# Turning the norm's deviations by TensorE, and comparing through a second tensor, in the patch-sorting stage of a four-layer network

## The chip, the cores and the metric

The kernel runs on one core of a Trainium2 chip. The metric is device time in microseconds of one execution, as the median of several runs. A profiled execution gives the trace from which all durations below are read. The engines are named as in the profile: PE is TensorE (matmul; PEld its weight loads), DVE is VectorE, ACT is ScalarE, POOL is GpSimd, SP is the queue that issues DMAs.

## What is computed

The input is four images of 128 channels by 64 x 64 pixels. Four layers follow one another. The change lies in the first, cut here to what matters:

```python
sm = final_scores.reshape(B, Hp, PS, Wp, PS).mean((2, 4)).reshape(B, Hp * Wp)
idx = jnp.argsort(-sm, axis=1)                 # 256 patches of 4 x 4 pixels, best first
...
x1 = x_re.transpose(0, 2, 1) + pe_re           # pixels in the order of their patches, plus a position
mu = x1.mean(-1, keepdims=True)
var = ((x1 - mu) ** 2).mean(-1, keepdims=True)
x1n = (x1 - mu) * jax.lax.rsqrt(var + 1e-05) * norm_g + norm_b
xz = x1n @ in_proj_w.T
...
_, ys = jax.lax.scan(step, h0, ...)            # a state-space scan along the 4096 pixels
...
inv = jnp.argsort(order, axis=1)               # the pixels go back to their places
```

The scores come from two depthwise convolutions with a channel attention. The norm is over the 128 channels of a pixel. The layers after it (a convolution, an attention, two expert feed-forwards and a linear attention) are not touched.

## The kernel before, in words

All tensors have the 128 channels on the partitions; a chunk is 512 pixels, eight to an image. For each image `in_order` prepares the sequence: a group norm, two depthwise convolutions on TensorE from patches that went through DRAM, the score of each patch, the sort, the norm, and the permutation of the patches by matmul. `scan` then runs the state-space scan over the image, in eight pieces of 512 columns. A piece has 8 groups (`g`) of two slots (`i`), so 16 slots, and an image 128.

The first image is prepared alone, with every engine free, and there the framework's scheduler places the instructions. From then on the order is written by hand: the scan of image b runs, and beside it `others(b)` prepares image b + 1 as a Python generator that is advanced by one turn in each slot (line 919, pace 1). During the scan of the last image the finished sequences of the first three are put back into place instead (`end`, `put_back`).

In each slot the order of issue is:

- if `i` is 0, VectorE's product `hs` of 128 x 2048 (L886), whose second input `b_ps` comes from PE through one PSUM buffer;
- ScalarE's two `decay` exponentials (L893), through two PSUM buffers;
- `K.flush()` (L895), which issues all that was put off with `later` in the slot before;
- VectorE's two scans (L897), then on GpSimd a small copy of the carry (L900) and the product `hs` by `c_sb`, 128 x 1024 (L901), then on PE the sums `y_ps` of an earlier group;
- one turn of the preparation, and last, if `i` is 0, the next `b_ps` on PE.

Around this, once in each piece, lie the steps of `enter` for the next piece: `xc_ps`, `dbc_ps`, `dt_ps` on PE, activations on ScalarE, `dt` and `sp_u` on VectorE (L799, L800; the profile puts them to L126, the line that calls what was put off), and three products of 128 x 1024 on GpSimd. `leave` closes a piece: `yt` on VectorE (L825) and GpSimd (L821), `out_ps` on PE. `K.bank` gives out PSUM banks in turn (three during the scan) and flushes early when none is free.

The part that changes, for chunk c of the norm:

- `ask` loads the position; `placed` adds it to the image on GpSimd (L612); `centred` subtracts the mean by a matmul (`pos_xc`), and ScalarE squares it (L628) and copies it into `xn`, sorted by place in the patch (L630);
- `varied` takes the mean of the squares by a matmul with the 128 x 128 matrix `K.mean`. Every partition of `pos_var` then holds the same variances, 512 columns. VectorE turns them in blocks of 32 x 32 (L642) and copies one column of each block into `spreads` (L643): 16 numbers per partition and chunk;
- after every fourth chunk ScalarE takes the root (L649) and VectorE the reciprocal (L654); then, chunk by chunk, VectorE turns the 16 numbers, each repeated over 32 columns, back into `ln_rs` of 128 x 512 (L659), and GpSimd multiplies `xn` by it in two halves (L669). `ln_rs` has one buffer for the first four chunks, and alternates with that of `ln_vt` for the last four;
- `turn` and `sorted_` then transpose and permute on PE, with VectorE's copy L691 between, which needs all of `xn`.

`sort` compares each score with all others. `before` (L581) and `perm` (L603) compare the constant row `K.col` of 256 numbers with one number per partition; `eq` and `beats` (L583, L585) have two inputs besides. `put_back` compares in the same form at L947. In each slot's turn the sort's VectorE instructions are issued directly, so they stand behind the slot's scans.

Of the kernel before, what the change touches and what calls it, by code (L numbers as in the profile page):

```python
# [9 lines left out]
F32 = mybir.dt.float32  # L10
F32R = mybir.dt.float32r
I32 = mybir.dt.int32
AF = mybir.ActivationFunctionType
ALU = mybir.AluOpType
# [3 lines left out]
P = 128  # L18
# [3 lines left out]
CH = 512  # L22
NCH = L // CH
# [6 lines left out]
class Common:  # L30
# [59 lines left out]
    def mm(self, out, lhsT, rhs, start=True, stop=True):  # L90
        self.nc.tensor.matmul(out, lhsT, rhs, start=start, stop=stop)  # L91
# [32 lines left out]
    def later(self, f, *args, **kw):  # L124

        self.late.append(lambda: f(*args, **kw))  # L126
# [144 lines left out]
def layers01(K, xd, dpool, w, w1):  # L271
# [3 lines left out]
    nc, tc, mm = K.nc, K.tc, K.mm  # L275
# [5 lines left out]
    with ExitStack() as ctx:  # L281
# [94 lines left out]
        deep1 = depthwise(w["conv1_w"], "deep1")  # L376
        deep2 = depthwise(w["conv2_w"], "deep2")
        rect = lambda t: t.rearrange("p (y x) -> p y x", x=HW)

        def image(b):  # L380
            t = big.tile([P, L], F32, name="xb", tag="mid")
# [6 lines left out]
        def staged(n, period, *stages):  # L388


            active, begun, turn = [], 0, 0
            while begun < n or active:
                if begun < n and turn >= begun * period:
                    active.append([begun, 0])
                    begun += 1
                for a in list(active):
                    if stages[a[1]] is not None:
                        stages[a[1]](a[0])
                    a[1] += 1
                    if a[1] == len(stages):  # L400
                        active.remove(a)
                turn += 1
                yield

        def together(*parts):

            parts = list(parts)
            while parts:
                for p in list(parts):
                    if next(p, True):  # L410
                        parts.remove(p)
                if parts:
                    yield

        def wait(n):
            for _ in range(n):
                yield
# [5 lines left out]
        def in_order(b, made, work, psum):  # L423
# [143 lines left out]
            def sort():  # L567
                yield from wait(6)
                sp = K.bank(psum, [P, 256], "sm_ps")
                mm(sp, share.to_broadcast([P, P]), sm)  # L570
                later(nc.vector.tensor_copy, sm, sp)
                yield from wait(2)
                beats = []
                for h in range(2):
                    dg = small.tile([P, P], F32, name="dg")
                    nc.vector.tensor_tensor(dg, sm[:, h * P : (h + 1) * P], K.ident, ALU.mult)
                    cl = small.tile([P, 1], F32, name="cl")
                    nc.vector.tensor_reduce(cl, dg, AX.X, ALU.add)

                    before = small.tile([P, 256], F32, name="before")  # L580
                    nc.vector.tensor_scalar(before, K.col, K.row[:, h : h + 1], None, ALU.is_gt)  # L581
                    eq = small.tile([P, 256], F32, name="eq", tag="rank_eq")
                    nc.vector.scalar_tensor_tensor(eq, sm, cl, before, ALU.is_equal, ALU.mult)  # L583
                    bt = small.tile([P, 256], F32, name=f"beats{h}")
                    nc.vector.scalar_tensor_tensor(bt, sm, cl, eq, ALU.is_lt, ALU.add)  # L585
                    beats.append(bt)
                    yield
                yield
                rp = K.bank(psum, [P, 256], "rank_ps")
                for h in range(2):  # L590
                    mm(rp, K.ones, beats[h], start=h == 0, stop=h == 1)
                rank = small.tile([P, 256], F32, name="rank", bufs=NB)
                kept["rank"] = rank
                later(nc.vector.tensor_copy, rank, rp)
                yield
                yield
                for h in range(2):
                    dg = small.tile([P, P], F32, name="dg")
                    nc.vector.tensor_tensor(dg, rank[:, h * P : (h + 1) * P], K.ident, ALU.mult)
                    cl = small.tile([P, 1], F32, name="cl")  # L600
                    nc.vector.tensor_reduce(cl, dg, AX.X, ALU.add)
                    pm = small.tile([P, 256], F32, name=f"perm{h}", tag=f"beats{h}")
                    nc.vector.tensor_scalar(pm, K.col, cl, None, ALU.is_equal)  # L603
                    perm.append(pm)
                    yield

# [24 lines left out]

                later(taken)

            spreads = small.tile([P, NCH, CH // 32], F32, name="spreads")

            def varied(c):
                vp = K.bank(psum, [P, CH], "pos_var")
                mm(vp, K.mean, squares.pop(c))

                def turned():  # L640
                    vt = work.tile([P, CH // 32, 32], F32, name="ln_vt", tag="vt", bufs=1)
                    nc.vector.transpose(vt.rearrange("p a b -> p (a b)"), vp)  # L642
                    nc.vector.tensor_copy(spreads[:, c].unsqueeze(2), vt[:, :, 0:1])  # L643
                    if c % 4 == 3:
                        later(root)

                def root():
                    at = spreads[:, c - 3 : c + 1]
                    nc.scalar.activation(at, at, AF.Sqrt, bias=K.eps5)  # L649
                    later(inverted)  # L650

                def inverted():
                    at = spreads[:, c - 3 : c + 1]
                    nc.vector.reciprocal(at, at)  # L654
                    turned_back(c - 3)

                def turned_back(n):
                    rs = work.tile([P, CH // 32, 32], F32, name="ln_rs", tag="vt" if n > 3 and n % 2 else "rs", bufs=1)
                    nc.vector.transpose(rs, spreads[:, n].unsqueeze(2).to_broadcast([P, CH // 32, 32]))  # L659
                    later(scaled, n, rs.rearrange("p a b -> p (a b)"))  # L660
                    if n < c:
                        if n > 3:
                            later(turned_back, n + 1)
                        else:
                            later(later, turned_back, n + 1)

                def scaled(n, rs):
                    for a in range(2):
                        nc.gpsimd.tensor_tensor(inner(n, a), inner(n, a), outer(rs, a), ALU.mult)  # L669

                later(turned)

            yield from together(tail, sort(), staged(NCH, 2, ask, None, placed, centred, None, varied))
            yield from wait(7)


            xq = big.tile([P, L + 3], F32, name="xq", tag=f"seq{b % 2}")
# [262 lines left out]
        def put_back(xb, om, rank, prep, psum):  # L940
# [3 lines left out]
            perm_inv, turned = [], {}  # L944
            for h in range(2):
                pi = small.tile([P, 256], F32, name=f"perm_inv{h}")
                nc.vector.tensor_scalar(pi, rank, K.row[:, h : h + 1], None, ALU.is_equal)  # L947
                perm_inv.append(pi)
            yield

# [1123 lines left out]
```

## Time and profile before

| what | us |
|---|---|
| median of 3 runs | 10186.19 |
| lowest and highest run | 10174.80 and 10188.59 |
| the profiled execution | 10174.38 |
| its span, first to last instruction | 10172.6 |
| preparation of the first image, up to the scan's first L886 | 281.6 |
| scan of images 1, 2, 3 and 4, from first L886 to the next one's | 612.8, 612.1, 614.7 and 650.9 |
| pieces 0 to 7 of the third image's scan | 65.9, 69.3, 74.2, 106.3, 100.6, 73.1, 62.7, 62.6 |

The last two rows were read off the starts of L886 in the trace. In pieces 1 to 3 the convolutions of the next image run beside the scan, in pieces 4 and 5 its sort, norm and permutation, in 6 and 7 nothing. Both other scans that have a preparation beside them show the same lengths within 4 us a piece.

How to read the lines that follow: a group line gives line, engine, operation, output and inputs, shapes and count, then total busy us, mean ns of one, and the idle time just before, with what ended it. A line of the order in time begins with start and duration in us. A line of windows gives the stretch, its length, the busy us and number of instructions of PE, PEld, DVE, ACT and POOL, the granted clock of TensorE, and the DMA share and rate.

### The profile page before, as it was taken

To read this page: it belongs to the slowest core of one execution; us is meant where nothing else is said; L and a number is where in the kernel's file an instruction comes from. 1 tells how busy PE (TensorE), PEld (TensorE's weight loads), DVE (VectorE), ACT (ScalarE), POOL (GpSimd) and SP (SyncE) were. 2 spreads that over 40 slices of the span, in tenths; PEclk is the share of its full clock that TensorE was granted. 3 is DMA by queue.
4 is the path that set the end of the run, shared out by engine and by line. 5 is a ranking of instruction groups with operands and counts; after the bars stand their busy time and mean duration, and the time that the engine had idled before them with its cause. 6 is when DMAs were issued, how large, how long until landed. Compare 5 with 4: busy or idle time off the path is not lost. (4 is left out here: it accounts for less than half of the span.)

```text
span 10172.6 us, 185611 instructions
## 1 busy us (share of the span) xinstructions
PE 8764.2 (86%) x72472; PEld 3315.3 (33%) x72472; DVE 7559.9 (74%) x8255; ACT 7361.3 (72%) x10542; POOL 4791.7 (47%) x3135
## 2 busy tenths in 40 slices
PE   5687887889859999969999969999979999967766
PEld 1122222235433333323333323333333333323433
DVE  1789797997748888868888768888778888753563
ACT  2666656654439999959999959999869999831531
POOL 0667576675515555545555545555445555420000
PEclk8787878889979999989999979999989999988987
DMA  5634536222222222142222142222132222123004
GB/s 125 154 77 104 130 77 149 65 75 76 77 64 36 41 42 38 29 110 35 42 40 39 29 111 35 42 38 39 28 112 38 39 39 40 36 94 118 0 18 149
DMA packets 629614, 669.26 MB, mean 66 GB/s; under 512 B 185400, under 2 KB 416896, under 8 KB 621568
## 3 DMA queue, kind: packets, MB, share of 16 engines
q1 hardware_dynamic: 628736, 657.39, 28.3%
q8 instruction: 571, 9.36, 0.4%
q14 instruction: 307, 2.51, 0.1%
HBM read 446.84 MB, written 143.13 MB: 58 GB/s over the span
## 5 line engine op out<-in xcount | busy, mean ns | idle before, releaser
L1491 ACT ACTIVATE ex<-score 128x1024 f32<-128x1024 f32 x5120 | 4928.0, 1037 | 176.2 <-PE score L91 89.1
L91 PE MATMUL ctx_ps<-ex,qt 128*32 128x512 f32 x20480 | 2735.6, 606 | 19.8 <-DVE ctx L1425 19.8
L1440 POOL TENSOR_TENSOR folded<-ex 128x1024 f32<-128x1024 f32 x512 | 1224.9, 2392 | 2124.8 <-ACT ex L1491 1857.4
L1497 DVE STREAM_TRANSPOSE turned<-ex 128x1024 f32<-128x1024 f32 x1536 | 1886.6, 1228 | 375.6 <-ACT ex L1491 278.6
L1473 DVE STREAM_TRANSPOSE turned<-ex 128x1024 f32<-128x1024 f32 x1532 | 1843.3, 1203 | 0.0
L91 PE MATMUL acc_ps<-turned,turned_v 128*32 128x256 f32 x24576 | 1769.5, 379 | 3.0 <-DVE turned L1503 3.0
L897 DVE TENSOR_TENSOR_SCAN hs<-decay,carry,hs 128x512 f32<-128x512 f32 x1024 | 1245.9, 1266 | 230.3 <-ACT decay L893 217.6
L91 PE MATMUL score<-queries,keys 32*128 32x512 f32 x10240 | 1334.9, 497 | 95.0 <-ACT ex L1491 44.4
L91 PEld LDWEIGHTS acc_ps<-turned,turned_v 128*32 128x32 f32 x24576 | 801.0, 110 | 1476.4 <-issue 1327.1
L901 POOL TENSOR_TENSOR hs<-hs,c_sb 128x1024 f32<-128x1024 f32 x512 | 1207.8, 2359 | 109.0 <-DMA c_sb<-c_d 69.0
L893 ACT ACTIVATE decay<-dt,a_neg 128x512 f32<-128x512 f32 x1024 | 694.3, 689 | 748.0 <-DVE hs L897 737.9
L91 PEld LDWEIGHTS score<-queries,keys 32*128 32x128 f32 x10240 | 512.9, 182 | 1191.8 <-ACT ex L1491 823.1
L1297 POOL TENSOR_TENSOR turned_v<-v,quarter 128x1024 f32<-128x1024 f32 x256 | 612.5, 2393 | 265.1 <-PE acc_ps L91 205.5
L91 PE MATMUL y_ps<-hs,pair 128*64 128x512 f32 x2048 | 663.8, 776 | 26.3 <-POOL hs L901 25.7
L1441 POOL TENSOR_TENSOR quarters<-folded 128x512 f32<-128x512 f32 x512 | 658.7, 1286 | 40.2
L886 DVE TENSOR_TENSOR hs<-dtx,b_ps 128x2048 f32<-128x2048 f32 x256 | 580.0, 2266 | 54.4 <-PE b_ps L91 29.7
L91 PEld LDWEIGHTS ctx_ps<-ex,qt 128*32 128x32 f32 x20480 | 406.5, 108 | 655.8 <-issue 599.7
L91 PE MATMUL b_ps<-dbc,state 32*64 32x512 f32 x1024 | 343.4, 753 | 218.0 <-DVE hs L886 217.8
L900 POOL COPY carry<-hs 128x2 f32<-128x2 f32 x512 | 97.9, 191 | 745.1 <-DVE hs L897 708.5
L1491 ACT ACTIVATION_READ_ACCUMULATOR ex<-score 128x1 f32 x2048 | 437.0, 213 | 0.0
L1425 DVE COPY ctx<-ctx_ps 128x512 f32<-128x512 f32 x256 | 177.0, 691 | 329.1 <-PE ctx_ps L91 316.2
L91 PE MATMUL conv<-under,deep 96*32 96x512 f32 x1536 | 216.7, 704 | 135.4 <-DMA under<-image_d 129.3
(360 smaller groups left out, 9390.6 us busy)
## 6 DMA issues: line engine op xcount, KB each, us to landing
c_sb<-c_d SPq DMA_DIRECT2D x512, 128.0 KB
queries<-head_d SPq DMA_DIRECT2D x1024, 64.0 KB
keys<-head_d SPq DMA_DIRECT2D x1024, 64.0 KB
under<-image_d SPq DMA_DIRECT2D x64, 792.0 KB
dt<-dt SPq DMA_DIRECT2D x128, 256.0 KB
dtx<-dtx SPq DMA_DIRECT2D x128, 256.0 KB
v<-value_d SPq DMA_DIRECT2D x1024, 32.0 KB
w<-in_L_ffn_weight SPq DMA_DIRECT2D x32, 1024.0 KB
```

Source lines behind the costliest of these rows:

```text
L91: self.nc.tensor.matmul(out, lhsT, rhs, start=start, stop=stop)
L886: nc.vector.tensor_tensor(hs, dtx2, bb.unsqueeze(1).to_broadcast([P, NQ, CH]), ALU.mult)
L893: nc.scalar.activation(ex, dt2[:, q, :], AF.Exp, scale=a_neg[:, q, g : g + 1])
L897: nc.vector.tensor_tensor_scan(hs[:, q, :], decays[q - 2 * i], hs[:, q, :], carry[:, g, q : q + 1], ALU.mult, ALU.add)
L901: nc.gpsimd.tensor_tensor(hs[:, two, :], hs[:, two, :], cs.unsqueeze(1).to_broadcast([P, 2, CH]), ALU.mult)
L1297: nc.gpsimd.tensor_tensor(t, v.unsqueeze(2).to_broadcast([P, 4 * BT, 4, HD]), quarter.unsqueeze(1).to_broadcast([P, 4 * BT, 4, HD]), ALU.mult,
L1425: nc.vector.tensor_copy(u, cps)
L1440: nc.gpsimd.tensor_tensor(hs, exs[:, :, 0], exs[:, :, 1], ALU.add)
L1441: nc.gpsimd.tensor_tensor(qs, hs[:, :, 0 : CH // 2], hs[:, :, CH // 2 :], ALU.add)
L1473: nc.vector.transpose(*upright)
L1491: nc.scalar.activation(ex, sps[p], AF.Exp, scale=scale, accum_out=sums[:, t : t + 1] if summed else None)
L1497: nc.vector.transpose(*upright)
```

## The change

There are two edits.

First, the norm. `varied` uses 32 columns of `K.mean` and four matmuls of 128 columns each, which write four groups of 32 partitions of a 128 x 128 bank: the 512 variances now lie over four groups of partitions, 128 columns wide, each repeated over the 32 partitions of its group. VectorE turns 128 columns in place of 512, into a buffer for four chunks; the copy L643 is gone, since ScalarE's root reads one column of each block out of that buffer itself. Root and reciprocal cover 4 numbers per partition and chunk in place of 16. The way back, L659, is gone: four matmuls multiply those numbers, one column repeated 128 times as weights, by the identity, and so spread them over all partitions into a bank `pos_rs`, from which ScalarE copies them to `ln_rs` in SBUF, now with a single buffer throughout. The multiplies on GpSimd are the same. A new generator `backs` paces these steps: two turns a chunk for the first four chunks, one for the last four.

Second, the comparisons `before`, `perm` and `perm_inv` (L581, L603, L947) are written as compare with the scalar, then multiply by a tensor of ones, in one instruction of two inputs.

```diff
+        ones256 = K.ones[:, 0:1].to_broadcast([P, 256])
...
-                    nc.vector.tensor_scalar(before, K.col, K.row[:, h : h + 1], None, ALU.is_gt)
+                    nc.vector.scalar_tensor_tensor(before, K.col, K.row[:, h : h + 1], ones256, ALU.is_gt, ALU.mult)
...
-                    nc.vector.tensor_scalar(pm, K.col, cl, None, ALU.is_equal)
+                    nc.vector.scalar_tensor_tensor(pm, K.col, cl, ones256, ALU.is_equal, ALU.mult)
...
-            spreads = small.tile([P, NCH, CH // 32], F32, name="spreads")
+            spreads = small.tile([P, NCH, 4], F32, name="spreads")
+            roots = [0]
             def varied(c):
-                vp = K.bank(psum, [P, CH], "pos_var")
-                mm(vp, K.mean, squares.pop(c))
+                vp = K.bank(psum, [P, P], "pos_var")
+                sq = squares.pop(c)
+                for k in range(4):
+                    mm(vp[32 * k : 32 * k + 32], K.mean[:, 0:32], sq[:, P * k : P * k + P])
                 def turned():
-                    vt = work.tile([P, CH // 32, 32], F32, name="ln_vt", tag="vt", bufs=1)
-                    nc.vector.transpose(vt.rearrange("p a b -> p (a b)"), vp)
-                    nc.vector.tensor_copy(spreads[:, c].unsqueeze(2), vt[:, :, 0:1])
+                    if c % 4 == 0:
+                        kept["vt"] = work.tile([P, 4, 4, 32], F32, name="ln_vt", tag="vt", bufs=1)
+                    nc.vector.transpose(kept["vt"][:, c % 4].rearrange("p a b -> p (a b)"), vp)
                     if c % 4 == 3:
                         later(root)
                 def root():
                     at = spreads[:, c - 3 : c + 1]
-                    nc.scalar.activation(at, at, AF.Sqrt, bias=K.eps5)
+                    nc.scalar.activation(at.unsqueeze(3), kept["vt"][:, :, :, 0:1], AF.Sqrt, bias=K.eps5)
                     later(inverted)
                 def inverted():
                     at = spreads[:, c - 3 : c + 1]
                     nc.vector.reciprocal(at, at)
-                    turned_back(c - 3)
-                def turned_back(n):
-                    rs = work.tile([P, CH // 32, 32], F32, name="ln_rs", tag="vt" if n > 3 and n % 2 else "rs", bufs=1)
-                    nc.vector.transpose(rs, spreads[:, n].unsqueeze(2).to_broadcast([P, CH // 32, 32]))
-                    later(scaled, n, rs.rearrange("p a b -> p (a b)"))
-                    if n < c:
-                        if n > 3:
-                            later(turned_back, n + 1)
-                        else:
-                            later(later, turned_back, n + 1)
-                def scaled(n, rs):
+                    roots[0] = c + 1
+                later(turned)
+            def scaled_by_root(n):
+                bp = K.bank(psum, [P, CH], "pos_rs")
+                by_block = bp.rearrange("p (g b i) -> p b g i", b=4, i=32)
+                for k in range(4):
+                    mm(by_block[:, k], spreads[:, n, k : k + 1].to_broadcast([P, P]), K.ident)
+                def taken():
+                    rs = work.tile([P, CH], F32, name="ln_rs", tag="rs", bufs=1)
+                    nc.scalar.copy(rs, bp)
+                    later(scaled, rs)
+                def scaled(rs):
                     for a in range(2):
                         nc.gpsimd.tensor_tensor(inner(n, a), inner(n, a), outer(rs, a), ALU.mult)
-                later(turned)
-            yield from together(tail, sort(), staged(NCH, 2, ask, None, placed, centred, None, varied))
-            yield from wait(7)
+                later(taken)
+            def backs():
+                for n in range(NCH):
+                    while roots[0] <= n:
+                        yield
+                    scaled_by_root(n)
+                    yield from wait(2 if n < 4 else 1)
+            yield from together(tail, sort(), staged(NCH, 2, ask, None, placed, centred, None, varied), backs())
+            yield
...
-                nc.vector.tensor_scalar(pi, rank, K.row[:, h : h + 1], None, ALU.is_equal)
+                nc.vector.scalar_tensor_tensor(pi, rank, K.row[:, h : h + 1], ones256, ALU.is_equal, ALU.mult)
```

The whole preparation of an image takes as many turns as before, and its early flushes fall in the same slots. In the built order each pair of xn products on GpSimd is issued one slot later than before in most chunks, the last pair in slot 8 of piece 5 in place of slot 7.

## The prediction

> **What bounds the kernel now.** I read the page first (busy shares, the 40 slices), then a table of windows cut at the starts of L886, which mark the 512-column pieces of the scan, then VectorE's groups in two of those windows, then the order in time of VectorE and GpSimd.
>
> ```profile
> PE 8764.2 (86%) x72472; PEld 3315.3 (33%) x72472; DVE 7559.9 (74%) x8255; ACT 7361.3 (72%) x10542; POOL 4791.7 (47%) x3135
> DVE  1789797997748888868888768888778888753563
> ```
>
> The averages say PE, but the change lies in slices 2 to 11, where VectorE stands at 7 to 9. The windows are pieces 4, 5 and 6 of the third image's scan, beside which the fourth image is prepared:
>
> ```profile
> 1822.20:1922.80 100.60, 73.86 (x162) 20.59 (x164) 91.10 (x83) 52.56 (x78) 63.32 (x48) 0.72 0.23 58
> 1922.80:1995.90 73.10, 62.77 (x210) 26.56 (x207) 69.97 (x60) 45.83 (x58) 59.31 (x49) 0.85 0.25 58
> 1995.90:2058.60 62.70, 50.23 (x150) 15.27 (x148) 59.99 (x47) 40.36 (x53) 47.08 (x35) 0.83 0.27 64
> ```
>
> Columns: length, then busy PE, PEld, DVE, ACT, POOL. A piece with no preparation takes 62.7 us with VectorE at 96%; the piece that holds sort and norm takes 100.6 at 91%, the next 73.1 at 96%. So VectorE sets the pace and most of what norm and sort put on it lengthens the span. Its groups in the first two windows:
>
> ```profile
> L897 DVE TENSOR_TENSOR_SCAN hs<-decay,carry,hs 128x512 f32<-128x512 f32 x65 | 79.5, 1264 | 2.3 <-ACT decay L893 1.7
> L886 DVE TENSOR_TENSOR hs<-dtx,b_ps 128x2048 f32<-128x2048 f32 x16 | 36.2, 2264 | 0.3 <-POOL carry L900 0.3
> L643 DVE COPY spreads<-ln_vt 128x16 f32<-128x16 f32 x8 | 8.8, 1096 | 0.3
> L659 DVE STREAM_TRANSPOSE ln_rs<-spreads 128x512 f32<-128x512 f32 x8 | 5.6, 703 | 1.3 <-POOL xn L669 1.2
> L642 DVE STREAM_TRANSPOSE ln_vt<-pos_var 128x512 f32<-128x512 f32 x8 | 5.5, 689 | 5.1 <-PE pos_var L91 5.1
> L581 DVE TENSOR_SCALAR before<-col,row 128x256 f32<-128x256 f32 x2 | 4.8, 2408 | 0.0
> L603 DVE TENSOR_SCALAR perm<-col,cl 128x256 f32<-128x256 f32 x2 | 4.5, 2274 | 0.1
> L654 DVE RECIPROCAL spreads<-spreads 128x64 f32<-128x64 f32 x2 | 1.1, 530 | 0.0
> ```
>
> A copy of 16 elements takes 1.10 us in the mean and 0.13 at its fastest; a comparison of 256 takes 2.3 to 2.4 and 0.33 to 0.34 at its fastest. The order in time says why:
>
> ```profile
> 1857.39 2.40 DVE L581 TENSOR_SCALAR before<-col,row 128x256 f32<-128x256 f32 x1
> 1859.82 1.28 DVE L583 SCALAR_TENSOR_TENSOR eq<-sm,cl,before 128x256 f32<-128x256 f32 x1
> ```
> ```profile
> 1857.30 2.34 POOL L901 TENSOR_TENSOR hs<-hs,c_sb 128x1024 f32<-128x1024 f32 x1
> 1859.60 1.22 POOL L612 TENSOR_TENSOR pe<-pe,xp 128x512 f32<-128x512 f32 x1
> ```
>
> The comparison ends 0.15 us after GpSimd's L901 (1859.64), and L583 ends 0.28 after GpSimd's L612 (1860.82): VectorE was held while GpSimd ran.
>
> **What the Trainium skill says.** "SBUF — State Buffer", section "SBUF: two separate sides": VectorE and GpSimd share a port pair as an exclusive lock, taken for a whole instruction by a VectorE operation in a two-port mode, or by one with two SBUF inputs against a GpSimd operation that reads SBUF. The lines above agree for both forms: L581 (one input) and L583 (sm and before, both in SBUF). "VectorE: DVE Perf Modes", section "The perf-mode tier table": fp32 tensor_scalar and tensor_copy in SBUF run two elements per cycle, two-tensor operations one. The trace agrees: 0.34 us for L581 free, 0.48 for L583 and L585.
>
> **The change part by part**, per image prepared beside the scan (three of four), on VectorE:
> - L643 goes: 8.8 us, all but about 1 of it waiting for the lock.
> - L659 goes, to TensorE and ScalarE: 5.6 busy and 1.2 idle before it.
> - L642 works on 128 columns. Rows of 512 (0.689) and of 1024 (1.203, L1473) give about 1.0 ns a column, so 0.30: 8 x 0.39 = 3.1 us.
> - The reciprocal covers 16 numbers in place of 64: estimate 0.2, 2 x 0.33 = 0.7.
> Together 19.4 us. The first transpose waits 5.1 us for PE's pos_var behind xc_ps, and the scan after it waits 0.94 for ScalarE's decays; both stay and swallow its 0.6. Left: 18.8.
> - The comparisons. The new form reads K.col and ones, both in SBUF, so by L583 it is held as before. It costs 0.15 more when it runs (0.484 against 0.33 to 0.34): 4 x 0.15 = +0.6. Ends: if a repeated column didn't take the second port, perm would fall by 2.27 - 0.48 = 1.8, twice, -3.6 (before gains nothing: L583 behind it would then wait); nothing in the trace suggests more than +0.6 above. I take +0.6. That leaves 18.2 on VectorE.
>
> Other engines. PE: pos_var becomes 8 instructions of 128 columns in four groups of output partitions; pos_rs adds 8 per chunk. A 512-column instruction starts 0.43 us after the one before in the fast stretches, 0.85 in the slow ones, so one of 128 costs 0.11 to 0.21 and pos_rs 0.9 to 1.9, 7 to 15 us an image. PE is busy 63 of 73 us there, much of it at the low clock (0.72 and 0.85 granted): covered, save for one wait below. ScalarE: 8 copies at 0.59 (row L960) = 4.7, on 46 of 73 us: covered if the copy needn't wait. No DMA changes and no wait count: the built order has the preparation end at the same turn (98) in both.
>
> GpSimd is where cover ends. Its work is unchanged, but each pair of xn multiplies is issued one slot later, since a PE step and a ScalarE step replace one transpose. A slot is two scans (2.45), with L886 (2.27) in every second one. In piece 5, slots 2 to 8, GpSimd already runs without a break:
>
> ```profile
> 1941.17 2.35 POOL L821 TENSOR_TENSOR yt<-yt,sz 128x1024 f32<-128x1024 f32 x1
> ...
> 1946.04 1.67 POOL L669 TENSOR_TENSOR xn<-xn,ln_rs 128x256 f32<-128x256 f32 x2
> ...
> 1960.49 2.35 POOL L901 TENSOR_TENSOR hs<-hs,c_sb 128x1024 f32<-128x1024 f32 x1
> ```
> ```profile
> 1961.21 2.71 DVE L126 TENSOR_TENSOR dt<-sp_u,dt 128x1024 f32<-128x1024 f32 x1
> ```
>
> A slot there costs GpSimd 2.55 (L900, L901) + 1.67 = 4.2 against VectorE's 3.6, and VectorE's dt of slot 8 (two SBUF inputs) already waits for GpSimd to end at 1962.84. I laid these slots out by hand with the new order. rs has one buffer, so ScalarE's copy n waits for xn n-1 on GpSimd, with the next slot's decays queued behind it, and VectorE's scans behind those. From the start of slot 2's L886 to the end of slot 8's scans I get 35.0 us; before it is 1932.59 to 1967.01, 34.4. So what VectorE loses in these slots (0.35 + 0.71 and 0.7 + 1.2 + 0.7 = 3.7) brings nothing: 18.2 - 3.7 - 0.6 = 13.9. At the piece's start xn 0 now stands ahead of the last pe addition on GpSimd; pos_xc and b_ps follow that addition on PE, and L886 waits for b_ps: 0 to 2 us, I take 0.9. Left: 13.0 an image, some 12 of them in piece 4.
>
> The first image is prepared alone. There the last four xn multiplies run back to back (1.67 each, 216.8 to 223.3); with one rs buffer each waits for a 0.6 copy, about 2.4. VectorE's tail before it gets shorter by about 2.5 us, from the copy held at 213.72 and the shorter transposes; but the first four finish later, since their copies queue behind ScalarE's other work. I take +3 (-1 to +6). L947 (putting back, 8 times) has the comparisons' +0.15: +1.
>
> Sum: 3 x -13 + 3 + 1 = -35 us. The profiled execution took 10174.38 us (span 10172.6): 10139 on its base. The median of the runs shown is 12 us above it, so 10151 there.
>
> **Rivals.**
> 1. VectorE's whole saving arrives because GpSimd doesn't fall behind: 3 x -18.2 + 4 = -51, 10135. For it: GpSimd is busy only 59 of 73 us. Against it: its unbroken run above.
> 2. The new comparisons aren't held (they don't do what the trace says of two inputs): a further 3 x -3.6 - 2 = -13, 10138. Against it: L583, and dg at 1890.94 (1.62 for 0.26).
> 3. GpSimd's lateness spreads back into piece 4 (e, dt and dtx lie at 1883.9 to 1897.4, 20 of 25 us busy): only the first four transposes' saving, about 5, and the 0.6 hold: 3 x -4.5 + 4 = -10, 10176.
> 4. Slower: the copy into the single rs stalls ScalarE, and with it the decays, in every chunk and not only in slots 5 to 7. The longest wait is one L901 with its carry copy and one xn pair, 4.2 us; 7 waits x 3 images = 21 x 4.2 = 88, less 51: +37, 10223. It becomes slower than the bound below from (51 + 20) / 21 = 3.4 us a wait. For it: decays stand right behind the copy. Against it: for chunks 0 to 3 the copies lie two slots apart.
>
> **How the numbers follow.** A measurement here tells about 0.2% (20 us) from no change. Forecast 0.50; rival 1 0.14; rival 2 0.10; rival 3 0.18; rival 4 0.08. Faster is forecast, 1 and 2: 0.74; the same is 3: 0.18; slower is 4: 0.08. The likeliest case alone is 10135 to 10166 (s2 to s8 stall 0 to 3 more, the first image -1 to +6, PE's wait 0 to 2). The range 10122 to 10180 takes in rivals 1, 2 and 3; its low end has 1 and 2 together.
>
> **What would show it.** VectorE's rows: no L643 or L659, the transposes at 0.30, the comparisons still near 2.3 to 2.6 (rival 2: near 0.5). Piece 4 near 88 us and piece 5 near 72; the other pieces unmoved. New idle time before L897 put down to ScalarE's decays, in slots 6 and 7, with ScalarE waiting for GpSimd's xn. I am wrong if piece 5 shrinks by over 4 us or grows, if piece 4 shrinks by under 8, or if the first image's preparation moves by over 6.

## The result, and the profile after

| | us | runs |
|---|---|---|
| before, in the same comparison | 10179.55 (10174.09 to 10193.21) | 7 |
| after | 10146.23 (10133.15 to 10159.53) | 7 |
| ratio | 0.9963, 95% interval 0.9953 to 0.9973 | |
| profiled execution, before and after | 10174.38 and 10153.48 | |
| its span, before and after | 10172.6 and 10151.7 | |

The change saves 33 us of the median where the prediction said 35. From the page of the kernel after, the lines that were shown of before, first the busy time of each engine, then VectorE's tenths over the 40 slices:

```profile
PE 8749.1 (86%) x72920; PEld 3331.9 (33%) x72920; DVE 7495.5 (74%) x8191; ACT 7369.4 (73%) x10574; POOL 4792.9 (47%) x3135
...
DVE  1779797887748888778888778888778888753563
```

VectorE lost 64 us of busy time (7559.9 to 7495.5), far more than the run got shorter: part of it has turned into waiting. The table of windows for pieces 4, 5 and 6 of the third image's scan (length, then busy PE, PEld, DVE, ACT, POOL, the granted clock, DMA):

```profile
1812.50:1900.30 87.80, 70.50 (x218) 21.97 (x220) 78.30 (x72) 51.98 (x80) 62.28 (x47) 0.75 0.27 67
1900.30:1970.40 70.10, 63.34 (x267) 29.97 (x264) 64.86 (x55) 49.08 (x65) 61.91 (x51) 0.95 0.26 61
1970.40:2033.00 62.60, 49.07 (x147) 15.15 (x147) 59.88 (x46) 40.38 (x53) 47.03 (x35) 0.81 0.27 63
```

Piece 4 went from 100.6 to 87.8 us, with VectorE's busy time down by 12.8. Piece 5 went from 73.1 to 70.1 although VectorE has 5.1 us less to do there: its share fell from 96% to 93%. Piece 6 did not move. The groups of VectorE that matter here, in pieces 4 and 5 together (the seventeenth L901 is the first of piece 6, which begins within the window by 0.01 us):

```profile
L912 DVE TENSOR_TENSOR_SCAN hs<-decay,carry,hs 128x512 f32<-128x512 f32 x65 | 79.4, 1261 | 7.3 <-ACT decay L908 6.6
L901 DVE TENSOR_TENSOR hs<-dtx,b_ps 128x2048 f32<-128x2048 f32 x17 | 38.5, 2264 | 0.7 <-PE b_ps L91 0.4 <-POOL carry L915 0.3
L582 DVE SCALAR_TENSOR_TENSOR before<-col,row,ones 128x256 f32<-128x256 f32 x2 | 5.0, 2524 | 0.0
L604 DVE SCALAR_TENSOR_TENSOR perm<-col,cl,ones 128x256 f32<-128x256 f32 x2 | 3.1, 1548 | 0.1
L600 DVE TENSOR_TENSOR dg<-rank,ident 128x128 f32<-128x128 f32 x2 | 2.6, 1289 | 0.0
L648 DVE STREAM_TRANSPOSE ln_vt<-pos_var 128x128 f32<-128x128 f32 x8 | 2.4, 295 | 4.5 <-PE pos_var L91 4.5
L584 DVE SCALAR_TENSOR_TENSOR eq<-sm,cl,before 128x256 f32<-128x256 f32 x2 | 1.8, 887 | 0.1
L659 DVE RECIPROCAL spreads<-spreads 128x16 f32<-128x16 f32 x2 | 0.5, 232 | 0.0
```

The copy into `spreads` and the way back are gone, the transposes take 0.295 us in place of 0.689, and the price is in the first row: the scans sat idle for 7.3 us where they had sat for 2.3. The comparison is still held by GpSimd. VectorE and GpSimd in order of time:

```profile
1844.80 2.51 DVE L582 SCALAR_TENSOR_TENSOR before<-col,row,ones 128x256 f32<-128x256 f32 x1
1847.35 1.29 DVE L584 SCALAR_TENSOR_TENSOR eq<-sm,cl,before 128x256 f32<-128x256 f32 x1
```
```profile
1844.69 2.34 POOL L916 TENSOR_TENSOR hs<-hs,c_sb 128x1024 f32<-128x1024 f32 x1
1846.99 1.36 POOL L613 TENSOR_TENSOR pe<-pe,xp 128x512 f32<-128x512 f32 x1
```

L582 ends at 1847.31, 0.28 after GpSimd's L916 (1847.03). The old form ended 0.15 after it: the same hold, with a slightly longer tail.

The new idle time is in piece 5. ScalarE and VectorE there:

```profile
1926.99 0.58 ACT L672 COPY ln_rs<-pos_rs 128x512 f32<-128x512 f32 x1 [3.92 <-POOL xn L677]
1927.48 1.31 ACT L908 ACTIVATE decay<-dt,a_neg 128x512 f32<-128x512 f32 x2
```
```profile
1928.21 2.46 DVE L912 TENSOR_TENSOR_SCAN hs<-decay,carry,hs 128x512 f32<-128x512 f32 x2 [1.58 <-ACT decay L908]
1932.39 2.46 DVE L912 TENSOR_TENSOR_SCAN hs<-decay,carry,hs 128x512 f32<-128x512 f32 x2 [1.72 <-ACT decay L908]
```

ScalarE's copy into the single `ln_rs` waits 3.92 us for GpSimd's multiply of the chunk before; the decays stand behind it, and VectorE's scans behind those. That is the stall that the prediction laid out by hand for these slots.

Where the 20.9 us by which the profiled span got shorter went, from the starts of L886 (L901 after):

| part | before | after | difference |
|---|---|---|---|
| preparation of the first image | 281.6 | 281.1 | -0.5 |
| pieces 4 and 5, images 1, 2, 3 | 171.7, 171.5, 173.7 | 160.7, 161.0, 157.9 | -37.3 |
| pieces 0 to 3, images 1, 2, 3 | 316.1, 314.8, 315.7 | 320.2, 316.9, 322.9 | +13.4 |
| pieces 6 and 7, the three together | 376.2 | 374.7 | -1.5 |
| scan of the last image, to the end of its last L897 (L912 after) | 656.2 | 658.2 | +2.0 |
| all behind it | 7395.2 | 7398.2 | +3.0 |

The change shows in pieces 4 and 5, 12.4 us an image. No changed instruction lies in pieces 0 to 3, and their length scatters from 313.3 to 330.1 over the profiles of this case (piece 3 alone from 101.8 to 106.3 in the kernel before, a little more than the 4 us named above). In piece 2 of the third image, which took 74.2 us before and 82.4 after, ScalarE waited 2.4 us for PE's convolution before and 10.0 after, and that convolution 2.9 and 6.3 for its DMA from `image_d`. So part of these 13 us need not be there in other executions, which fits medians that differ by more, 33. Whether the change has a share in them is not shown: the twelve pieces together take 946.5 to 954.2 us in the three profiles with the old norm and 950.4 to 963.1 in the eight with the new one.

### The profile page after: what moved, and what is told of

Read it like the earlier page. It is cut to its first block, busy times and chain, and to the rows that moved or that the text cites. A ratio compares the mean times of both kernels' runs of the same rounds, so it can differ in the third digit from the quotient of the medians.

```text
span 10151.7 us, 186504 instructions
## 1 busy us (share of the span) xinstructions
PE 8749.1 (86%) x72920; PEld 3331.9 (33%) x72920; DVE 7495.5 (74%) x8191; ACT 7369.4 (73%) x10574; POOL 4792.9 (47%) x3135
## 3 DMA queue, kind: packets, MB, share of 16 engines
q14 instruction: 307, 2.51, 0.1%
## 5 line engine op out<-in xcount | busy, mean ns | idle before, releaser
L912 DVE TENSOR_TENSOR_SCAN hs<-decay,carry,hs 128x512 f32<-128x512 f32 x1024 | 1245.2, 1264 | 251.2 <-ACT decay L908 238.2
L916 POOL TENSOR_TENSOR hs<-hs,c_sb 128x1024 f32<-128x1024 f32 x512 | 1207.1, 2358 | 113.2 <-DMA c_sb<-c_d 73.0
L901 DVE TENSOR_TENSOR hs<-dtx,b_ps 128x2048 f32<-128x2048 f32 x256 | 579.8, 2265 | 65.3 <-PE b_ps L91 35.8
```

What stands on the lines that cost most here:

```text
L901: nc.vector.tensor_tensor(hs, dtx2, bb.unsqueeze(1).to_broadcast([P, NQ, CH]), ALU.mult)
L912: nc.vector.tensor_tensor_scan(hs[:, q, :], decays[q - 2 * i], hs[:, q, :], carry[:, g, q : q + 1], ALU.mult, ALU.add)
L916: nc.gpsimd.tensor_tensor(hs[:, two, :], hs[:, two, :], cs.unsqueeze(1).to_broadcast([P, 2, CH]), ALU.mult)
```

## The experiments

All times stand against runs of the kernel before on the same chip. "4 + 5" is the length of pieces 4 and 5 of images 1, 2 and 3; before it is 171.7, 171.5 and 173.7, mean 172.3.

### The comparisons alone

The kernel before, with L581, L603 and L947 in their new form; the norm stays.

```diff
-                    nc.vector.tensor_scalar(before, K.col, K.row[:, h : h + 1], None, ALU.is_gt)
+                    nc.vector.scalar_tensor_tensor(before, K.col, K.row[:, h : h + 1], ones256, ALU.is_gt, ALU.mult)
```

> The kernel before with the comparisons alone in the new form, the norm as it was. My theory: an operation of two SBUF inputs is held by GpSimd as the old one-input form was, so L581 and L603 stay near 2.4 and 2.3 us beside the scan, 0.15 us longer each at most; pieces 4 and 5 together grow by 0 to 1 us an image, the ratio to the kernel before is 1.000 to 1.0003. Rival (the new form isn't held): perm falls to 0.48 us, pieces 4 and 5 shrink by 3.6 us an image, some 11 to 13 us in all, ratio 0.9988.

Measured: 10189.86 us (13 runs) against 10180.84, ratio 1.0007 (0.9999 to 1.0015). 4 + 5: 172.1, 172.0, 171.9. The two comparisons in the two pieces:

```profile
L582 DVE SCALAR_TENSOR_TENSOR before<-col,row,ones 128x256 f32<-128x256 f32 x2 | 5.1, 2540 | 0.0
L604 DVE SCALAR_TENSOR_TENSOR perm<-col,cl,ones 128x256 f32<-128x256 f32 x2 | 4.8, 2402 | 0.1
```

Each comparison is 0.13 us longer than in its old form (2.41 and 2.27), four to an image, and none is released. The two-step form brings nothing: with a repeated column of ones as its second input the comparison is held as before.

### The norm alone

The kernel after, with the three comparisons put back as in the kernel before.

> The changed kernel with the comparisons put back to the old form, so the norm's change alone. My theory: the whole gain is the norm's, ratio to the kernel before 0.9963 to 0.9966, pieces 4 and 5 together 160 to 161 us as in the changed kernel, or up to 1 us shorter. Rival (part of the gain is the comparisons'): 0.9975, pieces 4 and 5 together 164 us.

Measured: 10139.04 us (5 runs), ratio 0.9956 (0.9943 to 0.9970). 4 + 5: 159.2, 157.0, 156.9, mean 157.7, which is 14.6 below before. Both parts together explain the whole: 0.9956 and +0.0007 make 0.9963. The whole gain is the norm's. That 4 + 5 is 2.2 us shorter in the mean than in the kernel after is only 0.5 the comparisons' own. The rest is idle time of VectorE in small parts: 0.5 less before the first transpose, which waits for PE, 0.5 less at the start of piece 5, where VectorE's product waits for `b_ps` (2.32, 0.48 and 0.47 us in the three images here, 2.31, 2.31 and none after), and smaller ones elsewhere. The wait for `b_ps` is the one that jumps from image to image. In order of time, PE around it, and the window of these instructions, first in the kernel after (second image), then in this one (the column before the last two is the granted clock):

```profile
1289.41 2.08 PE L91 MATMUL pos_xc<-pe,center 128*128 128x512 f32 x2 [2.04 <-POOL pe L613]
1291.42 1.97 PE L91 MATMUL b_ps<-dbc,state 32*64 32x512 f32 x4
1289.41:1293.39 3.98, 3.98 (x8) 0.86 (x10) 1.77 (x2) 1.86 (x4) 3.90 (x4) 0.50 0.28 66
```
```profile
1287.52 1.13 PE L91 MATMUL pos_xc<-pe,center 128*128 128x512 f32 x2 [2.07 <-POOL pe L613]
1288.58 1.07 PE L91 MATMUL b_ps<-dbc,state 32*64 32x512 f32 x4
1287.52:1289.65 2.13, 2.13 (x8) 0.56 (x10) 1.76 (x2) 0.96 (x3) 2.05 (x2) 1.00 0.45 123
```

The same six instructions behind the same wait for GpSimd's addition take 3.98 us in one and 2.13 in the other. VectorE's L901 follows `b_ps`: it starts at 1293.49 after 2.31 us idle in the one (the profile names no releaser and says "issue"), at 1289.76 after 0.48 in the other. The Trainium skill, "TensorE: Matmul & The Clock Gate", section "What's actually happening", describes a gate that lets half of the pulses of PE's clock through after an idle window and all of them after a busy one, in windows that run freely, whatever the kernel does. These lines agree with the two rates: the granted clock is 0.50 in the one and 1.00 in the other, and the times stand as 1.87 to 1. Which window decides is not shown here; PE's idle time just ahead, 2.04 and 2.07 us, does not tell the two apart.

### The copy L643 on ScalarE, all else as in the kernel before

```diff
-                    nc.vector.tensor_copy(spreads[:, c].unsqueeze(2), vt[:, :, 0:1])
+                    nc.scalar.copy(spreads[:, c].unsqueeze(2), vt[:, :, 0:1])
```

> The kernel before with one line changed: the copy of 16 numbers, L643, on ScalarE in place of VectorE. My theory: 7.8 of the copy's 8.8 us an image are VectorE held by GpSimd, and ScalarE isn't held, so pieces 4 and 5 together shrink by 7 to 9 us an image, 21 to 27 in all, ratio 0.9974 to 0.9979. Rival (the copy is long for another reason, such as its stride, or its time was hidden): ScalarE takes as long or other waits take its place, pieces 4 and 5 shrink by 1 us or less, ratio 0.9997 or above.

Measured: 10159.35 us (16 runs), ratio 0.9980 (0.9973 to 0.9987). 4 + 5: 167.1, 166.7, 165.7, mean 166.5. On ScalarE the copy takes 0.216 to 0.220 us every time, never held. The Trainium skill, "SBUF — State Buffer", section "SBUF: two separate sides", says that only VectorE and GpSimd meet at the shared port pair; this agrees. VectorE is rid of 8.8 us an image, and the pieces are shorter by 5.8 in the mean (by 4.6, 4.8 and 8.0 in the three images). What is missing is in the main idle time ahead of two of VectorE's groups. Pieces 4 and 5 of the second image, first before, then here:

```profile
L897 DVE TENSOR_TENSOR_SCAN hs<-decay,carry,hs 128x512 f32<-128x512 f32 x65 | 79.5, 1264 | 1.9 <-ACT decay L893 1.3
L691 DVE COPY perm_s<-perm_t 128x512 f32<-128x512 f32 x7 | 4.7, 675 | 0.0
```
```profile
L897 DVE TENSOR_TENSOR_SCAN hs<-decay,carry,hs 128x512 f32<-128x512 f32 x65 | 79.3, 1260 | 4.5 <-ACT decay L893 3.9
L691 DVE COPY perm_s<-perm_t 128x512 f32<-128x512 f32 x7 | 4.7, 673 | 1.7 <-PE perm_t L687 1.7
```

Over the three images the scans wait 2.2 us longer in the mean, mostly for ScalarE's decays. The copies `perm_s` wait 1.6 to 1.7 us for PE in all three; in the kernel before they did so in the third image alone, which is one reason why that image gains most. So the costliest single line of the old norm is worth two thirds of its busy time: 5.8 of the 14.6 us that the norm alone saves in these pieces.

### Two buffers for `ln_rs` in the last four chunks

```diff
-                    rs = work.tile([P, CH], F32, name="ln_rs", tag="rs", bufs=1)
+                    rs = work.tile([P, CH], F32, name="ln_rs", tag="vt" if n > 3 and n % 2 else "rs", bufs=1)
```

> The changed kernel with two buffers for ln_rs in chunks 4 to 7 (alternating with that of ln_vt, as before the change). In the changed kernel VectorE idles 0.7 + 1.6 + 1.7 us in piece 5 for ScalarE's decays, which stand behind the copy into the single buffer. My theory, that GpSimd's queue is full in slots 2 to 8: the waits of ScalarE go, but VectorE then waits for GpSimd at dt or at perm_s instead, and piece 5 shrinks by less than 1.5 us. Rival (the single buffer itself is the cause): piece 5 shrinks by 3.5 to 4.5 us and no other wait of VectorE grows.

Measured: 10134.94 us (4 runs), ratio 0.9959 (0.9945 to 0.9972), which can't be told from the kernel after. 4 + 5: 157.9, 159.6, 157.8; piece 5: 70.1, 70.0, 70.0. From slot 2 to slot 8 VectorE now takes 32.0, 34.1 and 32.0 us in place of 35.0. But the piece as a whole stays at 70: PE waits for GpSimd, and VectorE for PE, a few slots later. First VectorE, then PE, then GpSimd:

```profile
1935.94 0.69 DVE L706 COPY perm_s<-perm_t 128x512 f32<-128x512 f32 x1 [2.42 <-PE perm_t L702]
```
```profile
1935.01 0.90 PE L702 MATMUL perm_t<-ident,xn 128*128 128x128 f32 x3 [5.60 <-POOL xn L677]
```
```profile
1929.22 1.23 POOL L915 COPY carry<-hs 128x2 f32<-128x2 f32 x1
1930.53 2.80 POOL L916 TENSOR_TENSOR hs<-hs,c_sb 128x1024 f32<-128x1024 f32 x1
1933.30 1.65 POOL L677 TENSOR_TENSOR xn<-xn,ln_rs 128x256 f32<-128x256 f32 x2
```

GpSimd runs without a gap over these lines. The wait through ScalarE was one form of GpSimd's lateness; taken away, it comes back through PE in the first and the third image. In the second, which had the wait for `b_ps`, VectorE is busy for 65.8 us of piece 5 in place of 63.6 instead, with a longer `sp_u`.

### The norm alone, with two buffers

> The changed kernel with the old comparisons and two buffers for ln_rs in chunks 4 to 7, so both earlier single edits together. If they add up, pieces 4 and 5 together fall from 159.9 (mean of the changed kernel) by 2.1 and 1.4 to 156.4, ratio to the kernel before 0.995. If the 2.1 came from the instant at which PE's clock was low and not from the comparisons, the sum lies anywhere from 156 to 159.

Measured: 10138.19 us (4 runs), ratio 0.9953 (0.9938 to 0.9968). 4 + 5: 158.5, 156.7, 159.5, mean 158.2: no shorter than the norm alone (157.7), so the two edits don't add. Why, is seen when the lengths of piece 5 are sorted by whether its first L901 waited for `b_ps` about 2 us or more (1.97 to 2.32). The wait itself lies ahead of the start of L901 and counts in piece 4; the table has what follows it, over all these kernels:

| `ln_rs` buffers, kernels | with that wait | with 0.5 us or less |
|---|---|---|
| one: after, norm alone, `before` made once (further below) | 71.8, 71.3, 71.6, 71.5 | 70.1, 70.3, 70.3, 70.2, 70.2 |
| two: this one, two buffers, all together (further below) | 70.0, 70.0, 70.5, 70.7 | 70.1, 70.1, 70.0, 70.4, 69.2 |

With one buffer the wait costs 1.3 us in the mean; with two it costs 0.3. Without the wait the second buffer brings 0.3. Piece 5 comes out near 70 us (69.2 at the lowest) whichever of these waits is taken away: that is the floor of this arrangement. The lines of the two-buffer kernel point to GpSimd; the next experiment says how far.

### Two turns a chunk for all chunks

```diff
-                    yield from wait(2 if n < 4 else 1)
+                    yield from wait(2)
```

> The changed kernel with two turns for each chunk of the way back, so in chunks 4 to 7 too; the preparation ends four turns later. Pieces 4 to 6 together take 223.3, 223.6 and 220.5 us in the changed kernel. My theory, that GpSimd is full in slots 2 to 8 of piece 5 because an xn pair falls into each of slots 5 to 8: now every second slot has one, GpSimd catches up, VectorE's idle time for ScalarE's decays goes, and pieces 4 to 6 shrink by 3 to 4.5 us an image. Rival (VectorE's loss there is the permutation's or ScalarE's own load, and only moves): pieces 4 to 6 change by less than 1 us.

Measured: 10171.52 us (17 runs) against 10183.0, ratio 0.9985 (0.9978 to 0.9992): most of the gain is lost, and neither theory's sum came true. Piece 5 is 70.1, 70.1 and 69.6, but piece 6, at 62.6 in the kernel after, is 70.7, 70.7 and 71.0. Windows of pieces 5 and 6 of the third image, and two of VectorE's groups in piece 6:

```profile
1913.94:1983.57 69.63, 56.52 (x213) 21.61 (x210) 63.01 (x50) 44.27 (x61) 60.15 (x51) 0.83 0.25 61
1983.57:2054.61 71.04, 58.66 (x201) 23.65 (x201) 62.43 (x51) 45.12 (x57) 47.19 (x35) 0.87 0.25 56
```
```profile
L912 DVE TENSOR_TENSOR_SCAN hs<-decay,carry,hs 128x512 f32<-128x512 f32 x33 | 40.0, 1264 | 4.9 <-ACT decay L908 4.6
L706 DVE COPY perm_s<-perm_t 128x512 f32<-128x512 f32 x5 | 3.4, 680 | 3.6 <-PE perm_t L702 3.6
```

The slower pace pushes the permutation four slots on, into a piece that had one copy of it. Its copies cost VectorE 2.7 us there (five in place of one), PE's late `perm_t` 3.6, and the scans wait 2.2 longer than in the kernel after (4.9 against 2.7 idle): 8.5, against the 8.4 by which the piece grew. Piece 5 gives back only 0.4 in this image, and 1.7 and 1.2 in the two that had the wait for `b_ps`. Slots 2 to 8 do shrink as the theory said, from 35.0 to 32.8 us in each image, and GpSimd even stands idle behind them, waiting for VectorE:

```profile
1954.12 0.19 POOL L915 COPY carry<-hs 128x2 f32<-128x2 f32 x1 [4.25 <-DVE hs L912]
```

Yet piece 5 stays at 69.6 to 70.1: `perm_s` now waits 3.6 us in it for `perm_t`, which needs the last pair of `xn`. So the 70 us are not GpSimd's load alone. It counts as well where in the order its last multiplies stand. Both theories had looked at the stall and not at where the steps behind it would land.

### The first step of the way back one turn later

```diff
                     while roots[0] <= n:
                         yield
+                    if n == 0:
+                        yield
```

> The changed kernel with one more turn ahead of the first step of the way back, so that xn 0 stands behind the last pe addition on GpSimd. In the changed kernel VectorE's product at the start of piece 5 idles 2.3, 2.3 and 0 us, and I hold that it waits for b_ps behind pos_xc behind that pe addition. My theory: this idle time falls to under 0.5 us in all three images, and pieces 4 and 5 shrink by up to 1.5 us; what they do not shrink by comes back in slots 5 to 9, as each later xn pair is one slot later as well. Rival (the wait has another cause, such as PE's extra matmuls): it stays or grows.

Measured: 10152.0 us (8 runs), ratio 0.9973 (0.9963 to 0.9984). 4 + 5: 158.9, 159.5, 160.1; piece 6 is 63.9 in all three. The idle time at the start of piece 5 is gone in every image, as the theory had it. But one product earlier, in piece 4, VectorE now waits (two lines of its order in time, with others between them left out):

```profile
1886.63 2.29 DVE L903 TENSOR_TENSOR hs<-dtx,b_ps 128x2048 f32<-128x2048 f32 x1 [2.15 <-PE b_ps L91]
...
1893.95 2.26 DVE L903 TENSOR_TENSOR hs<-dtx,b_ps 128x2048 f32<-128x2048 f32 x1
```

It is 1.72, 2.16 and 2.15 us in the three images, and in each two later products wait as well, 1.83 us in piece 5 and 1.73 in piece 6. So the order of these steps decides which product waits, as the theory said, but the wait has only moved, to other `b_ps`. On PE the first of them stands behind the eight new `pos_rs` instructions, so the rival's cause has a share there. Pieces 4 and 5 shrink by 1.8 and 1.5 us in the two images that had the wait and grow by 2.2 in the third, and piece 6 grows by 1.3 in all: no gain hangs on it.

### `before` made once for all images

The kernel after, with the two 128 x 256 matrices of L582, which are the same for every image, made ahead of all images.

```diff
+        earlier = cst.tile([P, 2, 256], F32, name="earlier")
+        for h in range(2):
+            nc.vector.tensor_scalar(earlier[:, h], K.col, K.row[:, h : h + 1], None, ALU.is_gt)
...
-                    before = small.tile([P, 256], F32, name="before")
-                    nc.vector.scalar_tensor_tensor(before, K.col, K.row[:, h : h + 1], ones256, ALU.is_gt, ALU.mult)
+                    before = earlier[:, h]
```

> The changed kernel with the matrices of the comparison before made once at the start (they are the same for every image) and not in each sort: two instructions of 2.51 and 2.55 us an image less on VectorE. My theory: they wait for GpSimd's running product, and the instruction behind them, eq, with two SBUF inputs, takes over that wait; pieces 4 and 5 together shrink by 1 to 2 us an image, and eq grows to 2.3 to 2.6 us. Rival (the time is the comparison's own): they shrink by 5 us and eq stays at 1.3 and 0.5.

Measured: 10148.23 us (5 runs), ratio 0.9963 (0.9950 to 0.9976), the same as the kernel after. 4 + 5: 159.4, 157.5, 157.5. An instruction of 2.52 us was taken out twice in an image, and the next in line took over its wait:

```profile
1851.27 2.42 DVE L586 SCALAR_TENSOR_TENSOR eq<-sm,cl,earlier 128x256 f32<-128x256 f32 x1
1853.73 0.48 DVE L588 SCALAR_TENSOR_TENSOR beats<-sm,cl,eq 128x256 f32<-128x256 f32 x1
```
```profile
1851.06 2.35 POOL L918 TENSOR_TENSOR hs<-hs,c_sb 128x1024 f32<-128x1024 f32 x1
```

`eq` lasted 1.29 and 0.48 us in the kernel after and lasts 2.41 in the mean here, to the end of GpSimd's product (1853.41) and 0.28 beyond, as in the lines of the result; `beats` grew by 0.40 in the mean. Of 5.05 us taken out, 3.9 came back (3.05 with `eq`, 0.81 with `beats`). The mean of 4 + 5 fell by 1.7: 1.2 that did not come back, and 0.6 less waiting of the products for `b_ps` (2 us in one image in place of two).

### The helpful edits together

The norm alone with two buffers, and `before` made once.

> The norm alone in its new form, with two ln_rs buffers for the last four chunks, and the matrices `before` made once for all images; the other comparisons stay in their old form. It joins the edits that each looked helpful alone. Theory (VectorE's two-input operations and GpSimd's work share one lock, so that an operation taken from VectorE hands its wait to the next such operation): eq takes over the waits of before (2.4 us a comparison, against 1.3 and 0.5), and the two pieces 4 and 5 of an image lie at 156 to 158 us, no more than 2 below the norm with two buffers (158.2); the run is 10125 to 10138. Rival (the savings add): 0.6 to 1.1 us for the buffers and 1.8 for before, added to the 157.7 of the norm alone, and with the waits of before gone too: 153 to 155 us, and a run below 10128.

Measured: 10126.27 us (5 runs) against 10178.82, ratio 0.9947 (0.9933 to 0.9960), the lowest of all; 4 + 5: 156.3, 158.1, 157.5, mean 157.3. The pieces say what the theory said: `eq` lasts 2.39 to 2.43 us, and the savings don't add. The time of the run does not decide, for it is within what both expected. It beats the kernel before by 0.53%; against the kernel after the interval overlaps (0.9953 to 0.9973), so that a gain of 0.16% is likely but not settled.

## Why the prediction was right, step by step

| step, per image if not said otherwise | predicted | measured |
|---|---|---|
| L643 and L659 leave VectorE | rows gone | rows gone |
| transpose of 128 columns | 0.30 us | 0.295 |
| reciprocals | -0.7 us | -0.6 (1.1 to 0.5) |
| each comparison, held as before | +0.15 us | +0.13 in the mean (the comparisons alone) |
| VectorE's busy time in pieces 4 and 5 | -17.6 us (8.8 + 5.6 + 3.1 + 0.7 - 0.6) | -18.1, -18.1, -18.0 |
| its idle time there | +4.6 us (the rest to -13.0) | +7.1, +7.7, +2.1 |
| slots 2 to 8 of piece 5 | 35.0 us (34.4 before) | 35.0 in all three images |
| wait for `b_ps` at the start of piece 5 | 0.9 (0 to 2) | 2.31, 2.31 and none |
| piece 4 | near 88 | 88.9, 89.7, 87.8 |
| piece 5 | near 72 | 71.8, 71.3, 70.1 |
| pieces 4 and 5 | -13.0 | -12.4 in the mean (-11.0, -10.5, -15.9) |
| first image's preparation, once | +3 (-1 to +6) | -0.5 |
| putting back, once | +1 | +1.1 of busy time (8 x 0.14, from the medians 0.452 and 0.590) |
| sum | -35 | -33 (medians) |

What carried it was to count the gain by stage and not by VectorE's busy time. Piece 4 pays nearly the whole of it, 11.5 us in the mean, and piece 5 hardly any, 1.0, because GpSimd, its work unchanged, has no slack in slots 2 to 8. The two-buffer kernels show by experiment that the stall at the single buffer is not what holds piece 5: it was taken away, and the piece stayed at 70 us. That GpSimd's multiplies are what holds it is read from the waits in the traces.

**Rivals.** That VectorE's whole saving would arrive falls with the 35.0 us of slots 2 to 8. That the comparisons would run free falls with 2.52 us for L582, and with the ratio 1.0007 of the comparisons alone. That the lateness would reach back into piece 4 falls with its 87.8 to 89.7. The slower case needed 21 waits of over 3.4 us of ScalarE's copy for GpSimd; the waits of ScalarE over all three images, with the sum, the number and the longest, are:

```profile
ACT ln_rs L672 <- POOL xn L677: 15.0, 7, 3.9
```

Seven in place of 21, 15.0 us in place of 88. Its mechanism is real, in the slots foreseen, and small. ScalarE's copy waited longer for PE's `pos_rs`, 29.0 us in 8 waits, which the prediction did not price: VectorE's next scans lost 0.4 to 0.6 us behind three of them and nothing behind the other five.

**What was wrong.** The first image's +3. Of its two halves the second was right: the last four pairs of `xn` now wait for the copy into the single buffer, 0.69 us each, 2.8 in place of the 2.4 assumed.

```profile
205.89 1.67 POOL L669 TENSOR_TENSOR xn<-xn,ln_rs 128x256 f32<-128x256 f32 x2 [0.61 <-ACT xn L630]
...
216.81 6.49 POOL L669 TENSOR_TENSOR xn<-xn,ln_rs 128x256 f32<-128x256 f32 x8 [1.21 <-DVE ln_rs L659]
```
```profile
202.74 1.66 POOL L677 TENSOR_TENSOR xn<-xn,ln_rs 128x256 f32<-128x256 f32 x2 [0.35 <-ACT ln_rs L672]
...
220.61 1.66 POOL L677 TENSOR_TENSOR xn<-xn,ln_rs 128x256 f32<-128x256 f32 x2 [0.69 <-ACT ln_rs L672]
```

These are GpSimd's multiplies before and after. The step "the first four finish later, since their copies queue behind ScalarE's other work" failed: the first pair starts 3.2 us earlier, and the last ends at 222.27 in place of 223.30. Neither the 3.2 nor the 1.0 at the end can be told from the scatter by one profile: the same preparation took 285.8 us with the comparisons alone and 277.9 with the norm and two buffers. So for the first image nothing is shown but that the loss is smaller than the scatter.

**What was right with a wrong size.** The `b_ps` wait of 0.9 does not occur in any image: over all these kernels it is near 2 us or at most 0.5, as PE's clock falls, and in the kernel after the image is at 161 us with it and at 158 without. In piece 4, the wait for `b_ps` at its end left out, VectorE's scans and products are idle 1.1 to 1.6 us longer than before (1.74 to 2.83, 2.83 and 3.36), mostly for ScalarE's decays; the prediction kept only the 0.94 that was there. That the transposes ahead of these scans became shorter is the likely reason, and was not tested. `perm` came out at 1.55 us in the third image and not at 2.4, since its place against GpSimd's work moved, and `dg` in turn at 1.29 for 0.94. And in the kernel before the third image, from which the prediction read its lines, held a wait in piece 5 that the other two did not have:

```profile
1981.89 0.69 DVE L691 COPY perm_s<-perm_t 128x512 f32<-128x512 f32 x1 [1.66 <-PE perm_t L687]
```

After the change 0.5 us of it is left there. So the -12.4 is a mean of -11.0 and -10.5, where the wait for `b_ps` is new, and -15.9, where it is absent and this other wait has shrunk. The errors are of both signs and larger than the 0.6 between -13.0 and -12.4: the size of VectorE's saving was foreseen, but the closeness of the sum is in part luck. So is that of the total, for the profiled execution after has +13.4 us in pieces 0 to 3, where no changed instruction lies.

**Open.** What halves PE's clock at the start of piece 5 in one image and not in the next, whether pieces 0 to 3 are really longer with the new norm, and whether the combined kernel is really faster than the one after, were not settled. A kernel with less work on GpSimd in piece 5, which would test the floor of 70 us from the other side, was not tried.

## What to carry to other kernels

When an engine holds the pace, ask stage by stage which engine is next, and lay that engine's instructions out for the slots that get shorter: a saving is paid only up to there, and here a stall removed short of that engine came back at another door. A VectorE instruction that is long because GpSimd holds the port pair is not a cost of its own: rewritten with two SBUF inputs it was held as before, and when `before` was taken out, the instruction behind it, `eq`, took over most of the wait. Where a scan stood behind it, as behind L643, the time was gained: the scans took 1.26 us in all these groups, and with that copy moved to ScalarE two thirds of its time came off the pieces. And when a hand-written order is slowed in one place, look first at where the steps behind it will land.

## What the runs showed of the hardware beyond that

- The hold works both ways, and on small instructions. In the two-buffer kernel GpSimd's copy of 2 columns took 1.23 us in place of 0.18, beside VectorE's `dt` of 1.22 us, which started 0.03 us before it:

```profile
1929.19 1.22 DVE L126 TENSOR_TENSOR dt<-sp_u,dt 128x1024 f32<-128x1024 f32 x1
```

- A second input that is one column repeated by a stride of zero does not spare an instruction the hold: L582 took 2.51 to 2.55 us with it beside the scan, and 0.48 us is the least that such a comparison took (`perm` of the first image after).
- PE's time for the same six instructions of 512 columns, behind an idle time of 2.04 or 2.07 us, was 3.98 us at a granted clock of 0.50 and 2.13 us at 1.00, in two kernels that differ on VectorE alone.
- Spreading one column over 128 partitions by a matmul with repeated weights costs little: the eight instructions of 128 columns of a chunk took 1.16 us at the end of piece 4 of the second image and 2.08 us there in the third, and all 256 of the program 40.0 us of PE's busy time. What they cost the span was not measured apart.
